# Selective-scan kernel: scans of 513 columns from a constant zero, the carried state in a column of the input

## The chip, the cores and the metric

The kernel runs on one core of one Trainium2 chip. The metric is device microseconds of one execution: the median of three runs. The core has five engines that work side by side and meet only at semaphores: PE (TensorE, matmuls), DVE (VectorE), ACT (ScalarE), POOL (GpSimd) and SP, which here only issues DMAs. Each of them takes its own instructions strictly in the order in which they were written.

## The reference

Two layers over an input of 4 x 512 x 4096 (batch, channels, positions). The first is a selective scan (Mamba) with residual, the second a linear attention with residual. The scan is run for each of four groups of 128 channels:

```python
dt = softplus(einsum(dt, dt_proj_w) + dt_proj_b)        # 256 inner channels
A = -exp(A_log)                                         # 256 x 16 states
def step(h, inp):
    dt_t, B_t, C_t, x_t = inp
    dA = jnp.exp(dt_t[:, :, None] * A)
    h = dA * h + (dt_t * x_t)[:, :, None] * B_t[:, None, :]
    y = jnp.einsum('bds,bs->bd', h, C_t)
    return h, y
```

In the second layer q and k pass a relu, `kq` is the sum over positions of k times q, and the output is `v @ kq`, normed, through an output matrix, plus the residual. Between them stand group norms and layer norms.

## The kernel before, in words

**Tiling.** A step is one image `b`, one tile `t` of T = 512 positions and one group `c` of 128 channels: 4 x 8 x 4 = 128 steps, with `c` innermost. In a step there are 256 inner channels with 16 states each, so 4096 recurrences over 512 positions. They are cut into 8 groups, one for each pair of half `e` and quarter `q` of the states. In a group, 128 partitions hold 32 channels x 4 states, and four blocks `j` of 32 channels stand side by side in the free dimension. So a group has four scans of 128 x 512, and the kernel has 1024 groups and 4096 scans. The carried state `st[:, c, e, q, j]` is needed four steps later, by the next tile of the same channels.

**A group, in two slots.** `slot(g)` writes half a group: two scans. The instructions of a group are these.
- `decay(k)` (L713, ACT): `dA = exp(d_all * a)`, 128 x 512, into PSUM. It is written three scans ahead (`LEAD = 3`), and each of the three `dA` tiles has a PSUM bank of its own.
- `drive(g)` (L721, POOL): `bx = d_all * b_all` for two scans, two slots ahead, in three buffers.
- The scan (L739, DVE): `h = dA * h + bx` along the 512 columns. It starts from `0.0` in the first tile of an image, and otherwise from the column `st[..., j]`.
- After a group's last scan POOL copies the last columns of the four blocks into `st` (L750) and multiplies the last quarter of `h` by `c_sb` (L751).
- `product` (L759, DVE): the first 384 columns of the four blocks, times `c_all`. It is written after the first scan of the next group.
- `c_row` (L705 through the helper at L124, PE): a bf16 matmul that spreads the row of C over the partitions into `c_all`, 384 columns of a PSUM bank. There is one such bank, so it comes after the product that read it last.
- `fold_states` (L772 through L124, PE): four matmuls that sum the states into `y`.

**The rest.** Each slot ends with `after()`, which writes a piece of everything else: the input projections and the short convolution of the step after next, the softplus and silu (with loads of ACT's tables), the spreading of `dt`, norms, output projections, and the attention of the image before. A credit of matmul work per slot sets how much. The order is written out by hand (`manual_schedule`), and the framework puts in the semaphore waits from the tiles that instructions read and write.

**PSUM.** Eight banks: one for `y`, one for `c_all`, three for `dA`, three for work.

Of the kernel before, what the change touches and what calls it, by code (L numbers as in the profile page):

```python
# [8 lines left out]
F32 = mybir.dt.float32  # L9
BF16 = mybir.dt.bfloat16  # L10
AF = mybir.ActivationFunctionType
ALU = mybir.AluOpType
AX = mybir.AxisListType

P = 128
T = 512
# [8 lines left out]
def kernel(  # L25
# [24 lines left out]
    nc = tc.nc  # L50
    B, C, L = x.shape
    NC = C // P
    NT = L // T
    DI = conv_b.shape[0]
# [3 lines left out]
    CUT = T - T // 4  # L58
    BLK = 32
    KS = P // BLK  # L60
    NQ = NST // KS
    NJ = P // BLK

    const = ctx.enter_context(tc.tile_pool(name="const", bufs=1))
    small = ctx.enter_context(tc.tile_pool(name="small", bufs=2))
    wk = ctx.enter_context(tc.tile_pool(name="wk", bufs=2))
    LEAD = 3

    dram = ctx.enter_context(tc.tile_pool(name="dram", bufs=2, space=bass.MemoryType.DRAM))
    ps_y = ctx.enter_context(tc.tile_pool(name="ps_y", bufs=1, space=bass.MemoryType.PSUM))  # L70
    ps_c = ctx.enter_context(tc.tile_pool(name="ps_c", bufs=1, space=bass.MemoryType.PSUM))
    ps_d = ctx.enter_context(tc.tile_pool(name="ps_d", bufs=LEAD, space=bass.MemoryType.PSUM))
    ps_w = ctx.enter_context(tc.tile_pool(name="ps_w", bufs=3, space=bass.MemoryType.PSUM))


# [45 lines left out]
    def mm(out_, lhsT, rhs, abreast=1, **how):  # L121

        work["mm"] += (0.25 if rhs.dtype == BF16 else 1.0) * rhs.shape[-1] / T / abreast
        nc.tensor.matmul(out_, lhsT, rhs, **how)  # L124
# [3 lines left out]
    def diagonal(out_, w, rhs):  # L128

        for k in range(P // BLK):  # L130
            r = slice(k * BLK, (k + 1) * BLK)
            mm(out_[r, :], w[r, :], rhs[r, :], abreast=P // BLK, start=True, stop=False)
# [56 lines left out]
    for i in range(1, 4):  # L189
        r = slice(i * LANE, (i + 1) * LANE)  # L190
# [10 lines left out]
    fold = const.tile([P, BLK], F32, tag="fold", name="fold")  # L201
    for k in range(KS):
        r = slice(k * BLK, (k + 1) * BLK)
# [18 lines left out]


    w_cv = const.tile([P, NTAP, DI], F32, tag="w_cv", name="w_cv")
    w_x = wk.tile([P, DI], F32, tag="bx", name="w_x", bufs=3)
    nc.scalar.dma_start(w_x, in_w[:, 0:DI])
    conv_bc = wk.tile([P, NTAP, DI], F32, tag="h", name="conv_bc", bufs=2)
    nc.scalar.dma_start(conv_bc, conv_w.partition_broadcast(P))
# [22 lines left out]
    for e in range(NH):  # L251
        r = e * (LANE + NST)
# [17 lines left out]


    bqk = const.tile([P, C], BF16, tag="bqk", name="bqk")
    b_qk = wk.tile([P, C], F32, tag="bx", name="b_qk", bufs=3)
    nc.vector.memset(b_qk, 0.0)
    for i in range(P // LANE):
        nc.scalar.dma_start(
# [6 lines left out]
    for i in (2, 3):  # L283
        r = slice(i * LANE, P)
# [7 lines left out]
    a_t = const.tile([P, NH, NJ, NQ], F32, tag="a_t", name="a_t")  # L292
# [82 lines left out]
    def bc(v, n):  # L375
        return v.unsqueeze(1).to_broadcast([P, n, v.shape[-1]])
# [190 lines left out]
    def shifted_end(f, name):  # L567
        mv = small.tile([P, NC, 2], F32, tag="mv", name=f"mv_{name}", bufs=4)
        for v in range(2):
            nc.vector.tensor_reduce(mv[:, :, v], f[("sum", "square")[v]], AX.X, ALU.add)  # L570
        nc.vector.tensor_scalar(mv, mv, 1.0 / L, None, ALU.mult)
        d2 = small.tile([P, NC], F32, tag="d2", name=f"d2_{name}")
        nc.vector.tensor_tensor(d2, mv[:, :, 0], mv[:, :, 0], ALU.mult)
        nc.vector.tensor_tensor(mv[:, :, 1], mv[:, :, 1], d2, ALU.subtract)
        nc.vector.tensor_tensor(mv[:, :, 0], mv[:, :, 0], f["mv"][:, :, 0], ALU.add)
        return mv
# [96 lines left out]
    JJ = NJ // 2  # L673
    SLOTS = NH * NQ * JJ
    AWAY = (3, 10)

    def place(g):

        n, r = divmod(g, SLOTS)
        e, r = divmod(r, NQ * JJ)  # L680
        return n, e, *divmod(r, JJ)

    b_all, c_all, c_sb, dAs, bxs, hs, ys = {}, {}, {}, {}, {}, {}, {}

    def for_states(dst, rows_, q):

# [5 lines left out]
    def b_row(g):  # L692
        n, e, q, _ = place(g)
        b_all[g // JJ] = wk.tile([P, T], F32, tag="b_all", name=f"b_all_{g}", bufs=3)
        for_states(b_all[g // JJ], fs[n]["b_rows"], q)

    def c_tail(g):
        n, e, q, _ = place(g)
        c_sb[g // JJ] = wk.tile([P, T - CUT], F32, tag="c_sb", name=f"c_sb_{g}", bufs=2)
        for_states(c_sb[g // JJ], fs[n]["c_rows"], q)  # L700

    def c_row(g):
        n, e, q, _ = place(g)
        got = ps_c.tile([P, CUT], F32, tag="c", name=f"c_all_{g}")
        mm(got, sel[:, q, :], fs[n]["parts"], start=True, stop=True)  # L705
        c_all[g // JJ] = got

    def decay(k):

        n, e, q, jj = place(k // 2)  # L710
        j = jj * 2 + k % 2
        dAs[k] = ps_d.tile([P, T], F32, tag="dA", name=f"dA_{k}")
        nc.scalar.activation(  # L713
            dAs[k], fs[n]["d_all", e][:, 0, j, :], AF.Exp, scale=a_t[:, e, j, q : q + 1]
        )

    def drive(g):

        n, e, q, jj = place(g)
        bxs[g] = wk.tile([P, 2, T], F32, tag="bx", name=f"bx_{g}", bufs=3)  # L720
        nc.gpsimd.tensor_tensor(  # L721
            bxs[g], fs[n]["d_all", e][:, 1, jj * 2 : jj * 2 + 2, :], bc(b_all[g // JJ], 2), ALU.mult
        )

    def slot(g, last, after):
        n, e, q, jj = place(g)
        b, t, c = steps[n]
        if g + 2 < last:
            drive(g + 2)
        if jj == 0:  # L730
            if g + 3 * JJ < last:
                b_row(g + 3 * JJ)
            hs[g // JJ] = wk.tile([P, NJ, T], F32, tag="h", name=f"h_{g}", bufs=2)
        elif g + 1 < last:
            c_tail(g + 1)
        h = hs[g // JJ]
        for i in range(2):
            j = jj * 2 + i
            nc.vector.tensor_tensor_scan(  # L739
                h[:, j, :], dAs.pop(2 * g + i), bxs[g][:, i, :],  # L740
                0.0 if t == 0 else st[:, c, e, q, j : j + 1], ALU.mult, ALU.add,
            )
            if 2 * g + i + LEAD < 2 * last:
                decay(2 * g + i + LEAD)
            if i == 0 and jj == 0 and g:
                product(g - 1)
                fold_states(g - 1, last)
        del bxs[g]
        if jj == JJ - 1:
            nc.gpsimd.tensor_copy(st[:, c, e, q, :], h[:, :, T - 1])  # L750
            nc.gpsimd.tensor_tensor(  # L751
                h[:, :, CUT:], h[:, :, CUT:], bc(c_sb.pop(g // JJ), NJ), ALU.mult
            )
        after()

    def product(g):

        own = hs[g // JJ][:, :, :CUT]
        nc.vector.tensor_tensor(own, own, bc(c_all.pop(g // JJ), NJ), ALU.mult)  # L759

    def fold_states(g, last):

        n, e, q, _ = place(g)
        if g + 1 < last:
            c_row(g + 1)
        if q == 0:
            ys[n, e] = ps_y.tile([P, T], F32, tag="y", name=f"y_{n}_{e}")
            diagonal(ys[n, e], dg[:, e, :], fs[n]["xz"][:, 0, e, :])
        h = hs.pop(g // JJ)
        for j in range(NJ):  # L770
            mm(
                ys[n, e][j * BLK : (j + 1) * BLK, :], fold, h[:, j, :],  # L772
                start=False, stop=(q == NQ - 1), abreast=NJ,
            )

# [30 lines left out]
    def attention(b, x1s, stats):  # L806
# [54 lines left out]
        for v in range(NT * SUB):  # L861
            t, u = divmod(v, SUB)
# [4 lines left out]
            for j in range(2):  # L867
                yield from room()
                i = 2 * v + j
# [24 lines left out]

        kqn = wk.tile([P, NC, P], F32, tag="res", name=f"kqn_{b}", bufs=2)
        nc.gpsimd.memset(kqn, 0.0)
        nrm = small.tile([P, NC], F32, tag="nrm", name=f"nrm_{b}")
        nc.vector.tensor_reduce(nrm, kq, AX.X, ALU.add)
        nc.vector.tensor_scalar(nrm, nrm, 1e-6, None, ALU.add)
        nc.vector.reciprocal(nrm, nrm)  # L900
        for i in range(P // HEAD):
            r = slice(i * HEAD, (i + 1) * HEAD)
# [22 lines left out]
        gr, _, ngm = norm  # L925
# [46 lines left out]
        for o in range(NC):  # L972
            for k in range(P // BLK):
                r = slice(k * BLK, (k + 1) * BLK)
# [31 lines left out]
    steps = [(b, t, c) for b in range(B) for t in range(NT) for c in range(NC)]  # L1006
    N = len(steps)
    names = [f"{b}_{t}_{c}" for b, t, c in steps]
    fs = [{} for _ in steps]
    xn, pads = {}, {}  # L1010
    norms, stats1, x1s = {}, {}, {}
    st = const.tile([P, NC, NH, NQ, NJ], F32, tag="st", name="st")

    def run(pieces):
        for _ in pieces:
            pass
# [14 lines left out]
    def leave(b, t):  # L1031
        if t == 0:
            stats1[b] = shifted_stats(b)
            x1s[b] = [
                dram.tile([P, NC, T], F32, tag="x1", name=f"x1_{b}_{i}", bufs=3 * NT)
                for i in range(NT)
            ]
        ym = xn[b, t][:, :, NTAP - 1 : NTAP - 1 + T]
        yield from projected(ym, stats1[b], x1s[b][t], b, t)
        if t == NT - 1:  # L1040
            add_to(rest, attention(b, x1s[b], stats1[b]))
# [40 lines left out]
    for g in range(JJ, 3 * JJ, JJ):  # L1082
        b_row(g)
    c_row(0)
    for g in range(2):
        drive(g)
    run(step_inputs(1))
# [6 lines left out]
    with tc.manual_schedule():  # L1094
        credit, seen, mix, held[0], held_x[0] = 0.0, work["mm"], iter(()), 0, 0
        for n, (b, t, c) in enumerate(steps):
            f, nm = fs[n], names[n]
# [9 lines left out]
            for s in range(SLOTS):  # L1107
                def after():
# [62 lines left out]
                    seen = work["mm"]  # L1171

                slot(n * SLOTS + s, N * SLOTS, after)
            fs[n - 1].clear() if n else None
        product(N * SLOTS - 1)
# [64 lines left out]
```

## Time and profile before

| | |
|---|---|
| time, median of three runs | 7947.49 us (7939.57 to 7963.91) |
| the profiled execution | 7963.09 us, span 7961.4 us |
| first scan to last scan | 122.4 to 7493.4 us |
| busy in the span | PE 81%, DVE 88%, ACT 69%, POOL 86% |
| mean granted TensorE clock | 0.897 |
| scan from a column (L739) | 3584 times, mean 1264 ns |
| scan from 0.0 (L739) | 512 times, mean 1203 ns |
| product (L759) | 1024 times, mean 1726 ns |
| exponential (L713) | 4096 times, mean 687 ns |
| `bx` (L721) | 2048 times, mean 2367 ns |

The durations overlap a little where instructions of one engine follow each other at once, so a sum of means is somewhat above the busy time. "Idle before, releaser" is time in which the engine had nothing running, and what ended it. The span falls in three parts: a head of 122 us in which the first inputs are made, the loop over the groups, and a tail of 468 us in which the attention of the last image is finished.

### The profile page before, as it was taken

How to read it: one execution, taken by the hardware profiler on the slowest of the kernel's cores; microseconds unless marked ns; L12 is line 12 of the kernel's file. 1: busy time of each engine (PE TensorE's matmuls, PEld its weight loads, DVE VectorE, ACT ScalarE, POOL GpSimd, SP SyncE). 2: the span in 40 equal slices, each digit the busy share in tenths (PEclk: the TensorE clock that was granted, in tenths of full speed). 3: DMA queues.
4: the chain of work that ended last, by engine and by line, in shares of the span. 5: the costliest groups of instructions: out<-in, count | busy, mean ns of one | idle time of the engine just before them, and what ended most of it. 6: DMA issues, size and time to landing. Idle time of an engine off the chain costs nothing.

```text
span 7961.4 us, 90563 instructions
## 1 busy us (share of the span) xinstructions
PE 6453.6 (81%) x24835; PEld 2120.0 (27%) x24880; DVE 6977.7 (88%) x5766; ACT 5507.6 (69%) x8321; POOL 6880.5 (86%) x4597
## 2 busy tenths in 40 slices
PE   5676777677789888888788888898688888888599
PEld 1121212112223222322222223332122332322144
DVE  5999999999999999989999999998999999988600
ACT  4667777777777777767777777677777777777421
POOL 4999999999999899989999899898999999889600
PEclk7888888888899999998899999899899999999799
DMA  5666666666666666777766666677666666676402
GB/s 154 167 168 166 151 155 159 160 155 167 169 179 162 151 163 159 174 189 175 174 155 171 171 157 161 155 185 189 156 167 163 161 161 159 145 194 180 112 32 90
DMA packets 829184, 1265.87 MB, mean 159 GB/s; under 512 B 183912, under 2 KB 317560, under 8 KB 816384
## 3 DMA queue, kind: packets, MB, share of 16 engines
q1 hardware_dynamic: 804736, 1222.32, 61.1%
q0 software_dynamic: 16896, 33.56, 2.4%
q10 hardware_dynamic: 7040, 4.20, 0.2%
q8 instruction: 195, 3.19, 0.2%
q14 instruction: 317, 2.60, 0.1%
HBM read 1052.78 MB, written 206.57 MB: 158 GB/s over the span
## 4 chain that ended last, share of the span: by engine, by line
DVE 33%; PE 21%; ACT 15%; DMA 12%; issue 8%; SPq 6%; POOL 6%; POOLq 0%; ACTq 0%; DVEq 0%
DVE h L739 22%; DVE h L759 9%; DMA d_all<-d_rows 7%; ACT dA L713 5%; PE pq L124 5%; POOL bx L721 4%; PE pc L124 4%; SPq L688 3%; PE y L124 3%; PE pr L124 3%; SPq L639 2%; DMA c_sb<-c_rows 2%; ACT xz L1048 2%; PE po L124 2%; ACT L1048 1%
## 5 line engine op out<-in xcount | busy, mean ns | idle before, releaser
L721 POOL TENSOR_TENSOR bx<-d_all,b_all 128x1024 f32<-128x1024 f32 x2048 | 4824.7, 2367 | 213.3 <-DVE h L739 195.1
L739 DVE TENSOR_TENSOR_SCAN h<-dA,st,bx 128x512 f32<-128x512 f32 x3584 | 4358.9, 1264 | 358.7 <-ACT dA L713 159.0
L713 ACT ACTIVATE dA<-d_all,a_t 128x512 f32<-128x512 f32 x4096 | 2752.9, 687 | 1568.5 <-DVE h L739 1521.8
L759 DVE TENSOR_TENSOR h<-h,c_all 128x1536 f32<-128x1536 f32 x1024 | 1767.5, 1726 | 0.1
L751 POOL TENSOR_TENSOR h<-h,c_sb 128x512 f32<-128x512 f32 x1024 | 1300.2, 1270 | 190.2 <-DMA c_sb<-c_rows 95.2
L124 PE MATMUL y<-h,fold 128*32 128x512 f32 x8192 | 1271.2, 696 | 71.6 <-POOL h L751 67.4
L124 PE MATMUL c_all<-parts,sel 128*128 128x384 bf16 x1024 | 369.9, 361 | 1123.3 <-DVE h L759 1121.7
L124 PE MATMUL pc<-xn,w_cv 128*128 128x512 f32 x2048 | 1045.7, 645 | 122.8 <-DVE xn L414 62.1
L124 PE MATMUL pq<-w_qk,xa 128*128 128x512 f32 x2048 | 965.5, 604 | 7.9 <-issue 5.3
L739 DVE TENSOR_TENSOR_SCAN h<-dA,bx 128x512 f32<-128x512 f32 x512 | 591.2, 1203 | 90.0 <-ACT dA L713 65.1
L124 PEld LDWEIGHTS <-sel 128*128 128x128 bf16 x1280 | 127.1, 99 | 1762.2 <-DVE h L759 1562.5
L124 PEld LDWEIGHTS pc<-xn,w_cv 128*128 128x128 f32 x2048 | 389.5, 201 | 747.1 <-issue 424.7
L124 PEld LDWEIGHTS pq<-w_qk,xa 128*128 128x128 f32 x2048 | 398.6, 196 | 439.6 <-issue 422.4
L124 PE MATMUL pr<-xb,m 128*128 128x512 f32 x1024 | 485.3, 612 | 7.5 <-DMA xb<-x 3.6
L124 PE MATMUL pp<-xn,w_pr 128*128 128x512 f32 x1024 | 477.7, 597 | 4.8 <-DVE xn L414 4.8
L124 PEld LDWEIGHTS y<-h,fold 128*32 128x32 f32 x8192 | 170.6, 114 | 644.0 <-issue 344.9
L124 PE MATMUL y<-xz,dg 32*32 32x512 f32 x2048 | 337.3, 734 | 0.0
L781 POOL TENSOR_TENSOR xz<-xz 128x512 f32<-128x512 f32 x256 | 325.7, 1272 | 9.2 <-ACT xz L778 9.2
L832 ACT ACTIVATE kq<-pq 128x512 f32<-128x512 f32 x256 | 150.5, 588 | 259.9 <-PE pq L124 259.2
L124 PE MATMUL pd<-xz,w_xp 128*128 128x512 f32 x512 | 323.4, 764 | 7.8 <-ACT xz L1048 7.8
L628 POOL TENSOR_TENSOR dt<-dt,xz 128x1024 f32<-128x1024 f32 x128 | 302.3, 2361 | 24.7 <-ACT dt L620 24.6
L124 PE MATMUL pz<-xn,w_z 128*128 128x512 f32 x512 | 275.4, 631 | 11.7 <-ACT xz L608 8.2
(179 smaller groups left out, 6034.1 us busy)
## 6 DMA issues: line engine op xcount, KB each, us to landing
d_all<-d_rows SPq DMA_DIRECT2D x2048, 256.0 KB, 6.7
b_all<-b_rows SPq DMA_DIRECT2D x4096, 64.0 KB, 2.2
d_rows<-dt SPq DMA_DIRECT2D x256, 512.0 KB, 3.6
c_sb<-c_rows SPq DMA_DIRECT2D x4096, 16.0 KB, 1.8
xs<-in_x_dram SPq DMA_DIRECT2D x32, 1024.0 KB, 6.3
xn<-in_x_dram SPq DMA_DIRECT2D x32, 1024.0 KB, 6.2
xr<-in_x_dram POOLq DMA_DIRECT2D x32, 1024.0 KB, 10.7
x<-xr SPq DMA_DIRECT2D x32, 1024.0 KB, 4.2
```

The lines of the kernel that those rows point to most:

```text
L124: nc.tensor.matmul(out_, lhsT, rhs, **how)
L628: nc.gpsimd.tensor_tensor(f["both"][:, 1], f["both"][:, 0], f["xz"][:, 0], ALU.mult)
L639: nc.sync.dma_start(d[k * BLK : (k + 1) * BLK, v], src)
L688: nc.sync.dma_start(dst[k * BLK : (k + 1) * BLK, :], rows_[q * KS + k, :].partition_broadcast(BLK))
L713: nc.scalar.activation(dAs[k], fs[n]["d_all", e][:, 0, j, :], AF.Exp, scale=a_t[:, e, j, q : q + 1])
L721: nc.gpsimd.tensor_tensor(bxs[g], fs[n]["d_all", e][:, 1, jj * 2 : jj * 2 + 2, :], bc(b_all[g // JJ], 2), ALU.mult)
L739: nc.vector.tensor_tensor_scan(h[:, j, :], dAs.pop(2 * g + i), bxs[g][:, i, :], 0.0 if t == 0 else st[:, c, e, q, j : j + 1], ALU.mult, AL ...
L751: nc.gpsimd.tensor_tensor(h[:, :, CUT:], h[:, :, CUT:], bc(c_sb.pop(g // JJ), NJ), ALU.mult)
L759: nc.vector.tensor_tensor(own, own, bc(c_all.pop(g // JJ), NJ), ALU.mult)
L781: nc.gpsimd.tensor_tensor(f["xz"][:, 1, e, :], f["xz"][:, 1, e, :], f["xz"][:, 0, e, :], ALU.mult)
L832: nc.scalar.activation(qk[i], pq, AF.Relu)
L1048: nc.scalar.activation(fs[n]["xz"], fs[n]["xz"], AF.Silu)
```

## The change

Every scan now covers 513 columns and starts from the constant 0.0. Ahead of `dA` stands a column that is always zero, and ahead of `bx` a column that holds the carried state, so the first column of the scan gives the state itself and the other 512 go on from it. For that
- the three `bx` buffers become one constant tile of three places of 2 x 513 columns;
- the three `dA` tiles and `c_all` become one PSUM tile of four banks, `banks`: `c_all` is columns 0 to 383, and three places of 513 columns stand at 509, 1022 and 1535;
- `h` has 513 columns in a block;
- ACT copies the carried state of a group into `bx` (`carry_in`, one or two copies), and its last columns out into `st` (`carry_out`) right after the group's last scan; in two of eight groups POOL does the copy out, and after the last tile of an image nobody does: POOL clears `st` instead;
- some small setup tiles move to other buffers.

```diff
-    ps_c = ctx.enter_context(tc.tile_pool(name="ps_c", bufs=1, space=bass.MemoryType.PSUM))
-    ps_d = ctx.enter_context(tc.tile_pool(name="ps_d", bufs=LEAD, space=bass.MemoryType.PSUM))
+    ps_d = ctx.enter_context(tc.tile_pool(name="ps_d", bufs=1, space=bass.MemoryType.PSUM))
...
+    RING, ROW = 3, T + 1
+    bx = const.tile([P, RING, 2, ROW], F32, tag="bx", name="bx")
+    banks = ps_d.tile([P, (LEAD + 1) * T], F32, tag="dA", name="banks")
+    dA_slots = banks[:, (LEAD + 1) * T - LEAD * ROW :].rearrange("p (s t) -> p s t", t=ROW)
...
-        got = ps_c.tile([P, CUT], F32, tag="c", name=f"c_all_{g}")
+        got = banks[:, 0:CUT]
...
-        dAs[k] = ps_d.tile([P, T], F32, tag="dA", name=f"dA_{k}")
+        dAs[k] = dA_slots[:, k % LEAD, :]
         nc.scalar.activation(
-            dAs[k], fs[n]["d_all", e][:, 0, j, :], AF.Exp, scale=a_t[:, e, j, q : q + 1]
+            dAs[k][:, 1:], fs[n]["d_all", e][:, 0, j, :], AF.Exp, scale=a_t[:, e, j, q : q + 1]
         )
...
+    def carry_in(g):
+        n, e, q, _ = place(g)
+        got = st[:, steps[n][2], e, q, :].rearrange("p (r i) -> p r i", r=JJ)
+        r = g % RING
+        if r + JJ <= RING:
+            nc.scalar.copy(bx[:, r : r + JJ, :, 0], got)
+        else:
+            for k in range(JJ):
+                nc.scalar.copy(bx[:, (r + k) % RING, :, 0], got[:, k, :])
+
+    def carry_out(g, copy):
+        n, e, q, _ = place(g)
+        b, t, c = steps[n]
+        if t < NT - 1:
+            copy(st[:, c, e, q, :], hs[g // JJ][:, :, T])
...
+        pooled = g % SLOTS in (AWAY[0], AWAY[1] + 1)
         for i in range(2):
             j = jj * 2 + i
             nc.vector.tensor_tensor_scan(
-                h[:, j, :], dAs.pop(2 * g + i), bxs[g][:, i, :],
-                0.0 if t == 0 else st[:, c, e, q, j : j + 1], ALU.mult, ALU.add,
+                h[:, j, :], dAs.pop(2 * g + i), bx[:, g % RING, i, :], 0.0, ALU.mult, ALU.add,
             )
+            if i == 1 and jj == JJ - 1 and not pooled:
+                carry_out(g, nc.scalar.copy)
             if 2 * g + i + LEAD < 2 * last:
                 decay(2 * g + i + LEAD)
+            if i == 0 and jj == JJ - 1 and g + 1 < last:
+                carry_in(g + 1)
...
         if jj == JJ - 1:
-            nc.gpsimd.tensor_copy(st[:, c, e, q, :], h[:, :, T - 1])
+            if pooled:
+                carry_out(g, nc.gpsimd.tensor_copy)
+            if t == NT - 1 and g % SLOTS == SLOTS - 1:
+                nc.gpsimd.memset(st[:, c], 0.0)
...
+    nc.vector.memset(st, 0.0)
+    nc.vector.memset(dA_slots[:, :, 0:1], 0.0)
```

More of the change, by code (lines that the diff above doesn't have):

```diff
@@ L224 @@
     w_cv = const.tile([P, NTAP, DI], F32, tag="w_cv", name="w_cv")
-    w_x = wk.tile([P, DI], F32, tag="bx", name="w_x", bufs=3)
+    w_x = wk.tile([P, DI], F32, tag="res", name="w_x", bufs=2)
     nc.scalar.dma_start(w_x, in_w[:, 0:DI])
@@ L272 @@
     bqk = const.tile([P, C], BF16, tag="bqk", name="bqk")
-    b_qk = wk.tile([P, C], F32, tag="bx", name="b_qk", bufs=3)
+    b_qk = wk.tile([P, C], F32, tag="res", name="b_qk", bufs=2)
     nc.vector.memset(b_qk, 0.0)
@@ L571, in shifted_end @@
         nc.vector.tensor_scalar(mv, mv, 1.0 / L, None, ALU.mult)
-        d2 = small.tile([P, NC], F32, tag="d2", name=f"d2_{name}")
+        d2 = small.tile([P, NC], F32, tag="d2", name=f"d2_{name}", bufs=1)
         nc.vector.tensor_tensor(d2, mv[:, :, 0], mv[:, :, 0], ALU.mult)
@@ L681, in place @@
         return n, e, *divmod(r, JJ)
-    b_all, c_all, c_sb, dAs, bxs, hs, ys = {}, {}, {}, {}, {}, {}, {}
+    b_all, c_all, c_sb, dAs, hs, ys = {}, {}, {}, {}, {}, {}
+    RING, ROW = 3, T + 1
+    bx = const.tile([P, RING, 2, ROW], F32, tag="bx", name="bx")
+    banks = ps_d.tile([P, (LEAD + 1) * T], F32, tag="dA", name="banks")
+    dA_slots = banks[:, (LEAD + 1) * T - LEAD * ROW :].rearrange("p (s t) -> p s t", t=ROW)
     def for_states(dst, rows_, q):
@@ L719, in drive @@
         n, e, q, jj = place(g)
-        bxs[g] = wk.tile([P, 2, T], F32, tag="bx", name=f"bx_{g}", bufs=3)
         nc.gpsimd.tensor_tensor(
-            bxs[g], fs[n]["d_all", e][:, 1, jj * 2 : jj * 2 + 2, :], bc(b_all[g // JJ], 2), ALU.mult
+            bx[:, g % RING, :, 1:], fs[n]["d_all", e][:, 1, jj * 2 : jj * 2 + 2, :], bc(b_all[g // JJ], 2), ALU.mult
         )
+    def carry_in(g):
[12 more added lines that the diff above has]
+            copy(st[:, c, e, q, :], hs[g // JJ][:, :, T])
     def slot(g, last, after):
@@ L732, in slot @@
                 b_row(g + 3 * JJ)
-            hs[g // JJ] = wk.tile([P, NJ, T], F32, tag="h", name=f"h_{g}", bufs=2)
+            hs[g // JJ] = wk.tile([P, NJ, ROW], F32, tag="h", name=f"h_{g}", bufs=2)
         elif g + 1 < last:
@@ L747, in slot @@
                 fold_states(g - 1, last)
-        del bxs[g]
         if jj == JJ - 1:
-            nc.gpsimd.tensor_copy(st[:, c, e, q, :], h[:, :, T - 1])
+            if pooled:
+                carry_out(g, nc.gpsimd.tensor_copy)
+            if t == NT - 1 and g % SLOTS == SLOTS - 1:
+                nc.gpsimd.memset(st[:, c], 0.0)
             nc.gpsimd.tensor_tensor(
-                h[:, :, CUT:], h[:, :, CUT:], bc(c_sb.pop(g // JJ), NJ), ALU.mult
+                h[:, :, 1 + CUT :], h[:, :, 1 + CUT :], bc(c_sb.pop(g // JJ), NJ), ALU.mult
             )
@@ L756, in product @@
     def product(g):
-        own = hs[g // JJ][:, :, :CUT]
+        own = hs[g // JJ][:, :, 1 : 1 + CUT]
         nc.vector.tensor_tensor(own, own, bc(c_all.pop(g // JJ), NJ), ALU.mult)
@@ L771, in fold_states @@
             mm(
-                ys[n, e][j * BLK : (j + 1) * BLK, :], fold, h[:, j, :],
+                ys[n, e][j * BLK : (j + 1) * BLK, :], fold, h[:, j, 1:],
                 start=False, stop=(q == NQ - 1), abreast=NJ,
@@ L896, in attention @@
         nc.gpsimd.memset(kqn, 0.0)
-        nrm = small.tile([P, NC], F32, tag="nrm", name=f"nrm_{b}")
+        nrm = small.tile([P, NC], F32, tag="nrm", name=f"nrm_{b}", bufs=1)
         nc.vector.tensor_reduce(nrm, kq, AX.X, ALU.add)
@@ L1084 @@
     c_row(0)
+    carry_in(0)
     for g in range(2):
```

## The prediction

> **What bounds the kernel now.** I read the page's busy shares first, then its costliest groups, then the loop by stages, then the order of time inside one group.
>
> ```profile
> span 7961.4 us, 90563 instructions
> ...
> PE 6453.6 (81%) x24835; PEld 2120.0 (27%) x24880; DVE 6977.7 (88%) x5766; ACT 5507.6 (69%) x8321; POOL 6880.5 (86%) x4597
> ...
> L721 POOL TENSOR_TENSOR bx<-d_all,b_all 128x1024 f32<-128x1024 f32 x2048 | 4824.7, 2367 | 213.3 <-DVE h L739 195.1
> L739 DVE TENSOR_TENSOR_SCAN h<-dA,st,bx 128x512 f32<-128x512 f32 x3584 | 4358.9, 1264 | 358.7 <-ACT dA L713 159.0
> L713 ACT ACTIVATE dA<-d_all,a_t 128x512 f32<-128x512 f32 x4096 | 2752.9, 687 | 1568.5 <-DVE h L739 1521.8
> ...
> L739 DVE TENSOR_TENSOR_SCAN h<-dA,bx 128x512 f32<-128x512 f32 x512 | 591.2, 1203 | 90.0 <-ACT dA L713 65.1
> ```
>
> Scans from a column take 1264 ns, those from 0.0 take 1203 ns. ACT waits 1522 us for scans; scans hardly wait for ACT (159 + 65 us). ACT runs ahead.
>
> The stages (columns: length, busy of PE, PEld, DVE, ACT, POOL):
>
> ```profile
> 122.40:7493.40 7371.00, 5968.01 (x23212) 1898.49 (x23240) 6913.61 (x5601) 5370.40 (x8110) 6865.96 (x4577) 0.90 0.67 166
> 7493.40:7961.40 468.00, 427.74 (x1494) 195.76 (x1510) 24.76 (x74) 103.85 (x167) 5.59 (x6) 0.94 0.18 59
> ```
>
> In the loop DVE is busy 94% and POOL 93%: 7371 / 1024 = 7.20 us a group. Head and tail together are 590 us.
>
> One group, in order of time (start, length):
>
> ```profile
> 2999.16 1.73 DVE L759 TENSOR_TENSOR h<-h,c_all 128x1536 f32<-128x1536 f32 x1
> ...
> 3000.81 4.80 DVE L739 TENSOR_TENSOR_SCAN h<-dA,st,bx 128x512 f32<-128x512 f32 x4
> ...
> 3000.95 0.34 PE L124 MATMUL c_all<-parts,sel 128*128 128x384 bf16 x1
> ...
> 3002.12 0.69 ACT L713 ACTIVATE dA<-d_all,a_t 128x512 f32<-128x512 f32 x1 [0.75 <-DVE h L739]
> ...
> 3003.30 0.69 ACT L713 ACTIVATE dA<-d_all,a_t 128x512 f32<-128x512 f32 x1 [0.48 <-DVE h L739]
> ...
> 3004.47 0.69 ACT L713 ACTIVATE dA<-d_all,a_t 128x512 f32<-128x512 f32 x1 [0.48 <-DVE h L739]
> ```
>
> Four scans follow each other without a gap, 1.175 us from start to start (those from 0.0: 1.115). The exponentials and the c_all matmul run **under** them. All of that rests on exponentials made three scans early, each in a tile of its own.
>
> **What the change removes.** 3584 scans lose the column operand: 60 ns each back to back, 215 us. The 513th column costs 1115 / 512 = 2 ns a scan, 9 us. POOL loses some 800 copies of 204 ns.
>
> **What it adds, and where.** ACT gets 1365 copies in and 672 copies out of four or two columns a partition. But the larger thing is not in the list of operations. The three places for dA and c_all are now columns of one tile, and in the program as built each wait is set on the last write to that tile, whichever columns it hit. I compared the waits: before, scan number i waits for exponential number i. After, it waits for exponential number i+2, in 3070 of 4096 scans; and that exponential is the one that waits for scan i-1. The second scan of a group (1023 of them) waits for c_row's matmul instead, which waits for the product; and the product (1023 of 1024) waits for the exponential written just before it. So the head start of three is gone: DVE, ACT, DVE, PE take turns. A chain, with nothing beside it but the other engines' other work.
>
> **The chain of one group.** From single records of the trace: a scan from 0.0 that starts after a wait takes 1224 ns, 1226 with the column; from its end to the start of a waiting exponential 35 ns; an exponential after idle time 692 ns; from its end to a waiting scan 33 ns. That makes 1.986 us, four times: 7.944. The product takes 1.726 back to back, 1.753 after a wait (a scan grows by the same 27 ns). From its end to c_all 57 ns; from a matmul's end to waiting DVE work 47 ns. The c_all matmul itself takes 336 ns in the median when PE was idle under 2 us before it, and 502 ns when it was idle over 5 us (29 records; 500 at 3 to 5 us, 145 records). PE will have 6 us of work in a group of over 10, so I take 502: 0.606 with the handovers. (The page TensorE: Matmul & The Clock Gate of the Trainium skill, Part 1, gives the reason: after an idle window of about 3.4 us the array's clock is halved. That PE would always be warm would make it 0.17 us a group less, 170 us in all.) The copy out stands in ACT's queue ahead of the group's last exponential and waits for its last scan; no row shows such a copy on ACT, the nearest are the accumulator reads of 128x1 (189 ns, 93 behind another instruction) and POOL's copy of the same four columns (204). It adds 0.1 to 0.2; I take 0.1, in 672 of 1024 groups: 0.07. The copies in run under a scan: nothing, as long as the scan covers them.
> Sum: 7.944 + 1.753 + 0.606 + 0.07 = **10.37 us** a group, 10,622 us in 1024.
>
> **What does not fit under the scans.** ACT's other instructions stand between the second and third and between the fourth and the next first exponential. What covers them is one scan with its handovers, 1.29 us, and 0.09 since back-to-back ACT instructions overlap. I counted ACT's instructions in each such gap of the changed program and priced them by their rows back to back. Most gaps hold 0.1 to 1.5 us. Two a step hold more: slot 3 with two table loads (1.283 each), two softplus (0.58) and others, 4.4 us; slot 10 with silu (1.911), two loads and others, 5.15 us. Their surplus is 3.0 + 3.8 us, in 128 steps 868 us; all other gaps give 166. Sum 1034. Even today's trace has such a place:
>
> ```profile
> 3018.24 1.28 ACT L1127 ACT_TABLE_LOAD   x1
> ...
> 3019.53 1.27 ACT L620 ACTIVATE dt<-pt,dtb 128x512 f32<-128x512 f32 x2
> ...
> 3020.82 1.28 ACT L1129 ACT_TABLE_LOAD   x1
> ...
> 3022.11 1.30 ACT L713 ACTIVATE dA<-d_all,a_t 128x512 f32<-128x512 f32 x2
> ...
> 3022.84 1.28 DVE L739 TENSOR_TENSOR_SCAN h<-dA,st,bx 128x512 f32<-128x512 f32 x1 [0.15 <-ACT dA L713]
> ```
>
> DVE's own other work runs while an exponential runs, 0.68 free: 93 norm products of 2.26 us stick out by 1.58, 48 pairs of statistics (1.35) by 0.67: 180 us.
> PE's queue: c_all now starts 0.86 us after the product in the mean, 0.06 in the median, because other matmuls stand ahead. Bounds 0 and 0.86 us a group, 0 to 885 us; with PE busy 50% in place of 81% I take 0.1, 100 us.
> POOL, 6.7 us a group, and the DMAs lie under 10.4 us: nothing.
>
> **Sum.** 590 + 10,622 + 1034 + 180 + 100 = 12,526 against a span of 7961; the runs' median is 0.2% below the profiled run, so **12,510 us**.
>
> **A rule that would cut it otherwise.** In the trace exponentials run during scans with each dA in a bank of its own. PSUM — Partial Sum Buffer of the Trainium skill (section PSUM bank collisions raise a hardware error) wants any two engines kept apart by bank, not by address. Places at 509, 1022 and 1535 straddle banks, so two neighbours share one, while the third place's exponential (1536 to 2047) shares none with the first place. By that rule alone a third of the exponentials could stay under the scan after them, and two thirds of those ahead of the product and of the c_all matmuls could stay hidden: 0.76 + 0.51 + 0.40 us a group less, an estimate of 10,800 us. No run here shows it; the waits as built go further.
>
> **The rivals.** (1) *Faster:* the head start survives. It decides if an exponential ends before the scan ahead of its own does. For it: today's 1522 us of ACT waiting. Against: the built waits. Then 215 us go from DVE, ACT's 2037 copies of at most 0.2 us fit, and POOL's loop falls to 6.7 ms: 7947 - 215 + 9 = 7740. (2) *Part of the chain is open,* so that only half of the 3.65 us a group of exponentials, c_all and handovers is in series (1.83 x 1024 = 1870 us less), or all of ACT's surplus is absorbed (1034 less): 10,640 to 11,480. (3) *PE late:* cold matmuls fill its queue and c_all keeps its 0.86 us: 13,300. (4) *The constant start gains nothing* and the head start holds: 7950.
>
> **How the numbers follow.** The chain 0.86, rival (1) 0.03, (2) 0.06, (3) 0.04, (4) 0.01. The chain's own range takes in no lateness and less surplus (11,900) and 0.7 us of lateness (13,200); it leaves out the rest. A change under about 0.3% could not be told from none. Faster 0.03, same 0.01, slower 0.96.
>
> **What would show it.** Right: scans single, 1.22 us, about 0.76 us of idle time before each with ACT's exponential as releaser, one in four released by PE; DVE busy near 57%, POOL near 55%; c_all near 0.5 us. Wrong: scans in rows of four without gaps, or exponentials under scans. If the time is near 11,500, look at the surplus of slots 3 and 10; if over 13,200, at PE ahead of c_all.

## The result, and the profile after

The changed kernel takes **12,449.9 us** (median of four runs, 12,448.2 to 12,455.87), the kernel before beside it 7948.06 us. The ratio is 1.566, with a 95% interval of 1.5635 to 1.5689. The prediction was 12,510 us in a range of 11,900 to 13,200. The profiled execution of after has a span of 12,446.5 us.

From the page of after: span, busy shares, and the groups that make the loop (line, engine, operation, tiles, shapes, count | busy us, mean ns | idle us before, releaser).

```profile
span 12446.5 us, 93106 instructions
...
PE 7601.4 (61%) x24831; PEld 2344.0 (19%) x24880; DVE 7225.2 (58%) x5768; ACT 5850.0 (47%) x10358; POOL 6692.7 (54%) x3813
...
L760 DVE TENSOR_TENSOR_SCAN h<-banks,bx 128x513 f32<-128x513 f32 x4096 | 5017.8, 1225 | 3525.1 <-ACT banks L716 2925.0
...
L716 ACT ACTIVATE banks<-d_all,a_t 128x512 f32<-128x512 f32 x4096 | 2825.9, 690 | 5284.0 <-DVE h L760 5263.2
L123 PE MATMUL banks<-parts,sel 128*128 128x384 bf16 x1024 | 413.3, 404 | 4123.7 <-DVE h L785 4123.4
L785 DVE TENSOR_TENSOR h<-h,banks 128x1536 f32<-128x1536 f32 x1024 | 1796.2, 1754 | 1187.2 <-ACT banks L716 1187.2
```

Read the idle columns against each other. The scans wait for the exponentials, the exponentials for the scans, the product for an exponential, and the c_all matmul for the product. It is a ring: each waits for the one that waits for it, so all of their durations add up. No engine is near full: DVE went from 88% to 58%, POOL from 86% to 54%, ACT from 69% to 47%.

The loop alone (stretch and length, then busy us of PE, PEld, DVE, ACT, POOL, granted clock, DMA share, GB/s):

```profile
123.50:11979.10 11855.60, 7115.60 (x23208) 2122.54 (x23240) 7161.03 (x5601) 5711.40 (x10144) 6675.39 (x3792) 0.77 0.42 103
```

Head (123.5 us) and tail (467.4 us) are as before. The loop takes 11,855.6 / 1024 = 11.58 us a group where it took 7.20. DVE's busy time in it hardly moved, from 6.75 to 6.99 us a group; its idle time went from 0.45 to 4.58. The waits of DVE in after (engine, tile and line that waits, what for: us in all, times, longest us) say where that sits:

```profile
DVE h L760 <- ACT banks L716: 2925.0, 2848, 48.1
DVE h L785 <- ACT banks L716: 1187.2, 1023, 8.6
DVE h L760 <- PE banks L123: 561.8, 1023, 2.9
```

These sum to 4674 us, or 4.56 us a group: all but 0.02 of the idle time.

The timeline of after (start and length in us, engine, line, operation, and the idle time before it with its releaser) shows slot 10 of a step first, and then one group:

```profile
6001.16 1.91 ACT L1076 ACTIVATE xz<-xz 128x2048 f32<-128x2048 f32 x1
...
6003.09 1.28 ACT L1178 ACT_TABLE_LOAD   x1
6004.39 0.69 ACT L716 ACTIVATE banks<-d_all,a_t 128x512 f32<-128x512 f32 x1
...
6005.11 1.22 DVE L760 TENSOR_TENSOR_SCAN h<-banks,bx 128x513 f32<-128x513 f32 x1 [4.44 <-ACT banks L716]
...
6008.41 0.69 ACT L716 ACTIVATE banks<-d_all,a_t 128x512 f32<-128x512 f32 x1 [1.35 <-DVE h L760]
6009.13 1.75 DVE L785 TENSOR_TENSOR h<-h,banks 128x1536 f32<-128x1536 f32 x1 [0.76 <-ACT banks L716]
6010.94 0.48 PE L123 MATMUL banks<-parts,sel 128*128 128x384 bf16 x1 [10.24 <-DVE h L785]
...
6011.45 1.22 DVE L760 TENSOR_TENSOR_SCAN h<-banks,bx 128x513 f32<-128x513 f32 x1 [0.57 <-PE banks L123]
6012.71 0.69 ACT L716 ACTIVATE banks<-d_all,a_t 128x512 f32<-128x512 f32 x1 [3.61 <-DVE h L760]
...
6013.51 1.23 DVE L760 TENSOR_TENSOR_SCAN h<-banks,bx 128x513 f32<-128x513 f32 x1 [0.83 <-ACT banks L716]
```

Add a start and a length and you have the next start, within some 0.1 us, down the whole group: 6008.41 + 0.69 gives 6009.10, and the product starts at 6009.13; 6009.13 + 1.75 gives 6010.88, and c_all starts at 6010.94. In the kernel before, the exponentials and c_all ran under the scans. The first four lines are a place where ACT has more to do than one scan covers: silu and a table load stand ahead of the exponential, and DVE stands still for 4.44 us.

### The profile page after: what moved, and what is told of

The parts are those of the page before. It is cut to its first block, busy times and chain, and to the rows that moved or that the text cites. A ratio compares the mean times of both kernels' runs of the same rounds, so it can differ in the third digit from the quotient of the medians.

```text
span 12446.5 us, 93106 instructions
## 1 busy us (share of the span) xinstructions
PE 7601.4 (61%) x24831; PEld 2344.0 (19%) x24880; DVE 7225.2 (58%) x5768; ACT 5850.0 (47%) x10358; POOL 6692.7 (54%) x3813
## 5 line engine op out<-in xcount | busy, mean ns | idle before, releaser
L760 DVE TENSOR_TENSOR_SCAN h<-banks,bx 128x513 f32<-128x513 f32 x4096 | 5017.8, 1225 | 3525.1 <-ACT banks L716 2925.0
L723 POOL TENSOR_TENSOR bx<-d_all,b_all 128x1024 f32<-128x1024 f32 x2048 | 4814.1, 2351 | 2663.9 <-DVE h L760 2592.7
L716 ACT ACTIVATE banks<-d_all,a_t 128x512 f32<-128x512 f32 x4096 | 2825.9, 690 | 5284.0 <-DVE h L760 5263.2
L123 PE MATMUL banks<-parts,sel 128*128 128x384 bf16 x1024 | 413.3, 404 | 4123.7 <-DVE h L785 4123.4
L785 DVE TENSOR_TENSOR h<-h,banks 128x1536 f32<-128x1536 f32 x1024 | 1796.2, 1754 | 1187.2 <-ACT banks L716 1187.2
L777 POOL TENSOR_TENSOR h<-h,c_sb 128x512 f32<-128x512 f32 x1024 | 1210.0, 1182 | 1679.1 <-ACT st L743 886.3
L123 PE MATMUL y<-h,fold 128*32 128x512 f32 x8192 | 1612.7, 871 | 3.6 <-DVE h L785 3.6
L123 PE MATMUL pc<-xn,w_cv 128*128 128x512 f32 x2048 | 1246.8, 751 | 315.4 <-DVE xn L413 150.7
L743 ACT COPY st<-h 128x4 f32<-128x4 f32 x672 | 132.3, 197 | 768.9 <-DVE h L760 766.6
L123 PE MATMUL y<-xz,dg 32*32 32x512 f32 x2048 | 422.6, 909 | 0.0
L123 PE MATMUL pd<-xz,w_xp 128*128 128x512 f32 x512 | 406.2, 938 | 7.8 <-ACT xz L1076 7.8
L807 POOL TENSOR_TENSOR xz<-xz 128x512 f32<-128x512 f32 x256 | 323.6, 1264 | 3.2 <-ACT xz L804 3.2
```

Source lines behind the costliest of these rows:

```text
L716: nc.scalar.activation(dAs[k][:, 1:], fs[n]["d_all", e][:, 0, j, :], AF.Exp, scale=a_t[:, e, j, q : q + 1])
L723: nc.gpsimd.tensor_tensor(bx[:, g % RING, :, 1:], fs[n]["d_all", e][:, 1, jj * 2 : jj * 2 + 2, :], bc(b_all[g // JJ], 2), ALU.mult)
L743: copy(st[:, c, e, q, :], hs[g // JJ][:, :, T])
L760: nc.vector.tensor_tensor_scan(h[:, j, :], dAs.pop(2 * g + i), bx[:, g % RING, i, :], 0.0, ALU.mult, ALU.add,)
L777: nc.gpsimd.tensor_tensor(h[:, :, 1 + CUT :], h[:, :, 1 + CUT :], bc(c_sb.pop(g // JJ), NJ), ALU.mult)
L807: nc.gpsimd.tensor_tensor(f["xz"][:, 1, e, :], f["xz"][:, 1, e, :], f["xz"][:, 0, e, :], ALU.mult)
```

## The experiments

The theory is that the lost head start is the whole loss: places that are columns of one tile make each scan wait for the exponential written last, and c_all in the same tile adds a turn of PE. The rivals are a cost of what else the change does (513 columns, the constant start, ACT's copies and their place in the queue) and a cost of the places themselves (banks that are straddled or shared). Each ratio below is to the kernel before, in the same set of runs.

**One tile, nothing else (e2).** The kernel before, with its three bank-sized places as columns of one PSUM tile:

```diff
-    ps_d = ctx.enter_context(tc.tile_pool(name="ps_d", bufs=LEAD, space=bass.MemoryType.PSUM))
+    ps_d = ctx.enter_context(tc.tile_pool(name="ps_d", bufs=1, space=bass.MemoryType.PSUM))
...
+    banks = ps_d.tile([P, LEAD * T], F32, tag="dA", name="banks")
...
-        dAs[k] = ps_d.tile([P, T], F32, tag="dA", name=f"dA_{k}")
+        dAs[k] = banks[:, (k % LEAD) * T : (k % LEAD + 1) * T]
```

> The kernel before, with one edit: the three dA places, each still 512 columns and exactly one bank, are columns of one PSUM tile of three banks. No 513th column, no copies on ACT, c_all in its own tile. My theory (waits are set on the last write to the tile, and that takes the head start): scan, exponential, scan take turns except under the product: 0.76 us three times a group and scans at their isolated 1.28 us, 8.95 us a group, with some 890 us of ACT's surplus, 180 of DVE's other work and 590 of head and tail: about 10800 us (10400 to 11200). Rival (columns that straddle banks, or ACT's copies, are what is slow): 7950 us.

Measured: 10,909.33 us, ratio 1.371 (1.3685 to 1.374). Its group of scans from a column:

```profile
L740 DVE TENSOR_TENSOR_SCAN h<-banks,st,bx 128x512 f32<-128x512 f32 x3584 | 4590.6, 1281 | 2719.9 <-ACT banks L714 2680.9 <-PE pd L124 9.8 <-POOL st L751 9.0
```

The same computation on three places of one bank each, with no copies on ACT and no 513th column, loses 2952 us against the 7956.87 us of before in its set. Each place still has a bank of its own, so no shared or straddled bank is needed for this part of the loss. The trace shows the wait itself: at the start of 4094 of the 4096 scans of e2 the exponential for the scan two further on has already ended, and so it is in after. In before that holds for 675 scans.

**A head start of one and of two (e8, e9).** If what is lost is the head start, then taking it away openly, with a tile for each place, must give the same. The kernel before, with one line changed (in e9 it is `LEAD = 2`):

```diff
-    LEAD = 3
+    LEAD = 1
```

> The kernel before with LEAD = 1: one dA tile of one bank, exponentials written one scan ahead. Nothing is shared, but a scan and the exponential of the next one must take turns, as in the run with three places in one tile (10909 us). My theory (the loss is the head start and nothing about the tile, its banks or the memory): the same chain, 10900 us, within 100. Rival (something about places in a common tile costs of itself): clearly under 10800 us.

> The kernel before with LEAD = 2: two dA tiles. It shows whether the two places in the runs with c_all of its own, with own places and in their control cost anything. My theory (one scan of 1.2 us covers an exponential of 0.69, but not ACT's table loads): 7960 to 8400 us. Rival (two places are already the loss seen there): about 10000 us.

Measured: e8 10,920.37 us, ratio 1.3725 (1.3697 to 1.3752); e9 8687.29 us, ratio 1.0918 (1.0896 to 1.094). The scans of e8:

```profile
L739 DVE TENSOR_TENSOR_SCAN h<-dA,st,bx 128x512 f32<-128x512 f32 x3584 | 4591.1, 1281 | 2724.4 <-ACT dA L713 2692.7 <-POOL st L750 9.0 <-PE pd L124 8.1
```

Set this beside e2's line: 1281 ns in both, 2719.9 and 2724.4 us idle, and times 0.1% apart. Three places in one tile behave as one place. That settles the main step. What e9 adds was a miss: two places cost 0.73 ms, above the 450 us that was the most expected. Its scans wait 730 us for exponentials where those of before wait 224, and 208 us for POOL's work on `h` and `st` where before they wait 10. So the third place is worth something beyond covering one exponential. The 367 waits for exponentials last 2.0 us in the mean, longer than one exponential; it seems that the third place takes up the lumps in ACT's other work, but that was not tested. What the waits for POOL come from was not separated.

**c_all out of the tile (e3).** The changed kernel, with c_all in a bank and tile of its own; the banks then leave room for two places instead of three:

```diff
-    LEAD = 3
+    LEAD = 2
...
+    ps_c = ctx.enter_context(tc.tile_pool(name="ps_c", bufs=1, space=bass.MemoryType.PSUM))
...
-        got = banks[:, 0:CUT]
+        got = ps_c.tile([P, CUT], F32, tag="c", name=f"c_all_{g}")
```

> The changed kernel with c_all in a bank and tile of its own again, and two dA places (LEAD = 2) in one tile of three banks to make room for it. My theory (c_all's share of the chain is the exponential ahead of the product and the matmul ahead of the second scan, 0.76 + 0.61 us a group and part of ACT's surplus): about 10850 us (10500 to 11250). Rival (the exponentials alone make the loss, c_all's waits were covered): 12300 to 12450 us.

Measured: 10,808.8 us, ratio 1.3586 (1.3559 to 1.3613). Its group of scans:

```profile
L761 DVE TENSOR_TENSOR_SCAN h<-banks,bx 128x513 f32<-128x513 f32 x4096 | 5010.7, 1223 | 3251.8 <-ACT banks L717 3200.3 <-issue 18.3 <-PE pc L124 10.0
```

The scans' wait for c_all is gone. So the two shared things split the loss: the places in one tile about 2.9 ms (with the rest of the change in it; e2, without that, loses 2.95), c_all in that tile another 1.64 ms (12,449.9 - 10,808.8), 1.60 us a group. That this tile has two places and not three should not matter, since e2 and e8 show that places of one tile behave as one.

**The copies out on POOL (e4).** The changed kernel, with every copy out on POOL and none on ACT:

```diff
-        pooled = g % SLOTS in (AWAY[0], AWAY[1] + 1)
+        pooled = True
```

> The changed kernel with every copy of the state out of h on POOL, as before the change, in place of ACT in six of eight groups. My theory (such a copy costs the chain about 0.1 us in 672 groups): 12385 us, 0.5% under the changed kernel. Rival (the copies on ACT, which stand ahead of the exponentials, are a main part of the loss): under 11800 us.

Measured: 12,405.29 us, ratio 1.5597 (1.5571 to 1.5623), 45 us (0.4%) less than after. The copy out is a small term of the chain and no cause of the loss.

**The constant start alone, the copies out on ACT alone, both (e1, e5, e10).** Three variants of the kernel before, all with its three tiles. e1 and e10 leave out the carried state: they show what the start from a column costs and could not replace the kernel.

e1 has the first edit, e5 the second, e10 both.

```diff
-                0.0 if t == 0 else st[:, c, e, q, j : j + 1], ALU.mult, ALU.add,
+                0.0, ALU.mult, ALU.add,
```

```diff
+            if i == 1 and jj == JJ - 1 and g % SLOTS not in (AWAY[0], AWAY[1] + 1):
+                nc.scalar.copy(st[:, c, e, q, :], h[:, :, T - 1])
...
-            nc.gpsimd.tensor_copy(st[:, c, e, q, :], h[:, :, T - 1])
+            if g % SLOTS in (AWAY[0], AWAY[1] + 1):
+                nc.gpsimd.tensor_copy(st[:, c, e, q, :], h[:, :, T - 1])
```

> The kernel before, with all scans started from the constant 0.0; the carried state is left out (POOL still copies it out). My theory (the loss comes from the waits on the shared tile, and the constant start itself is worth about 60 ns a scan): 3584 scans x 60 ns = 215 us less if DVE alone binds, less where POOL (93% of the loop) takes over: 7735 to 7850 us. Rival (the constant start is worth nothing): 7950 us.

> The kernel before with one part of the change alone: in six of eight groups ACT, not POOL, copies the last columns of h into st, behind the last scan and ahead of the exponential written there. My theory (the waits are what costs; a copy on ACT is covered by the head start of three, and POOL, 93% busy in the loop, gets 768 x 0.2 = 154 us free): the same or faster by up to 100 us, 7850 to 7960. Rival (a copy in ACT's queue that waits for the scan holds up the exponentials even with the head start): 8000 us or more.

> The kernel before with all scans from 0.0 (the carried state is left out) and in six of eight groups ACT in place of POOL copying the last columns out. Scans from 0.0 alone gave 0.94% where 215 us were at stake. My theory (POOL became the bound; 154 us of its copies go to ACT): 7780 to 7850 us, 1.2 to 2.1% under the kernel before. Rival (the rest of the gain was lost elsewhere, in PE's or ACT's waits): 7880 us, as with the scans alone.

Measured: e1 7881.34 us, ratio 0.9906 (0.9891 to 0.992); e5 7952.58 us, 0.999 (0.9981 to 0.9999); e10 7880.74 us, 0.9902 (0.9886 to 0.9919). e5 came as expected; e1 lies 31 us above its range, and e10 came out at its rival's number. The copy on ACT costs nothing while ACT runs ahead. The constant start did take its time from DVE: the scans' mean falls from 1264 to 1204 ns and DVE's busy time by 202 us. But only about 75 us (0.94%) reach the end. The rest turned into waits. The two waits of the scans in e1 (what for: us in all, times, longest us):

```profile
DVE h L739 <- POOL bx L721: 139.2, 127, 5.0
DVE h L739 <- PE y L124: 86.1, 85, 5.6
```

The same two in e10, where they change places:

```profile
DVE h L739 <- PE y L124: 163.0, 144, 5.0
DVE h L739 <- POOL bx L721: 95.2, 86, 5.1
```

In before these two are 78.0 us (POOL) and 90.8 us (PE). A faster DVE waits for POOL; where POOL is relieved of copies too, it waits for PE, and the time is the same. The loop before is so nearly balanced that much of the time saved on one engine reappears as waiting for another. Which of them holds the end was not settled: the expectation that POOL alone does fell with e10.

**A head start, with the change otherwise kept (e6, e7).** e6 is the changed kernel with two places in tiles of their own and c_all in its own bank. A place of 513 columns in a tile of its own takes two PSUM banks. With a bank for `y`, one for c_all and the three for work kept, only one such place fits; the other is in SBUF. To make room, `b_all` has two buffers in place of three.

```diff
-    banks = ps_d.tile([P, (LEAD + 1) * T], F32, tag="dA", name="banks")
-    dA_slots = banks[:, (LEAD + 1) * T - LEAD * ROW :].rearrange("p (s t) -> p s t", t=ROW)
+    dA_slots = [
+        ps_d.tile([P, 2 * T], F32, tag="dA", name="dA_psum")[:, 0:ROW],
+        const.tile([P, ROW], F32, tag="dA_sbuf", name="dA_sbuf"),
+    ]
...
-        got = banks[:, 0:CUT]
+        got = ps_c.tile([P, CUT], F32, tag="c", name=f"c_all_{g}")
```

e7 is its control: the kernel before with exactly these places, at 512 columns, from the column, with POOL's copy.

> The changed kernel (513 columns, constant zero, copies on ACT) with the sharing taken away: two dA places (LEAD = 2), one in a PSUM tile of two banks, one in an SBUF tile, each its own tile; c_all in its own bank; b_all two buffers and loaded two groups ahead, to make room. My theory (with places of their own the waits go back to the scan's own exponential): scans in rows without gaps again, 1.12 us from start to start out of PSUM, and 7800 to 8700 us, the upper end if scans with both inputs in SBUF disturb POOL. Rival (513 columns, straddled banks or the copies make the loss themselves): over 11000 us.

> The kernel before with the same two dA places as in the run with own places (512 columns; one in PSUM, one in SBUF, LEAD = 2, b_all two buffers), scans from the column, the copy out on POOL: what the places alone cost. My theory: 7950 to 8800 us, and the run with own places 50 to 200 us under this one, by the 60 ns a scan and POOL's lost copies. Rival (the 513th column and ACT's copies cost more than the constant start gains): the run with own places is slower than this one.

Measured: e6 10,095.83 us, ratio 1.2689 (1.2669 to 1.2709); e7 10,047.79 us, 1.2636 (1.2618 to 1.2654). Both far above what was expected. The scans of e6:

```profile
L763 DVE TENSOR_TENSOR_SCAN h<-dA_sbuf,bx 128x513 f32<-128x513 f32 x2048 | 4696.1, 2293 | 0.0
...
L763 DVE TENSOR_TENSOR_SCAN h<-dA_psum,bx 128x513 f32<-128x513 f32 x2048 | 2458.9, 1201 | 575.3 <-issue 180.6
```

The head start did come back: no idle time before the scans from SBUF, DVE busy 89%. But DVE is now busy with scans that are nearly twice as long when both inputs lie in SBUF. e7, without any of the change, has the same:

```profile
L743 DVE TENSOR_TENSOR_SCAN h<-dA_sbuf,st,bx 128x512 f32<-128x512 f32 x1792 | 4061.4, 2266 | 0.0
```

So the pair does not tell what the change would be worth with its head start of three; between themselves, under this slower DVE, the edits of the change come to 48 us more, where 50 to 200 us less were expected. A version with three places of 513 columns in separate PSUM tiles was not tried: at two banks each, beside `y` and c_all, they leave no bank for work. No complete version clearly faster than the kernel before came out of the runs; e5, the nearest, is 0.1% below it.

## Why the prediction was right, point by point

**The waits.** The step from which everything followed, that the places lose their head start because they are columns of one tile, is shown by e2 and e8, and the turn of PE by e3. It came from the waits of the built program; the list of operations alone would have given the first rival's 7740.

**The bank rule.** PSUM — Partial Sum Buffer of the Trainium skill (section PSUM bank collisions raise a hardware error) separates engines by bank; by that alone the estimate was 10,800 us. The 12,449.9 us measured are the built waits' number, and e2 loses its time with each place in a bank of its own. By that estimate two thirds of the exponentials ahead of the product would have stayed hidden; in after 1023 of 1024 wait for an exponential (1187.2 us), whichever place it writes. What straddled banks would cost with the waits gone was not tried.

**The terms.** A scan after a wait was put at 1226 ns and measures 1225, an exponential at 692 and 690, the product at 1753 and 1754. From the third scan of a group to the fourth it was to be 1.986 us, and the median is 1.985. The copy out was taken at 0.1 us: from the fourth scan to the next it takes 2134 ns in the median with the copy on ACT and 2039 ns with it on POOL, so 95. Two terms missed, and that they nearly cancelled was luck:
- c_all was put at 502 ns; its median is 476 and its mean 404, the handover to the scan 37 where 47 was taken. Its lateness behind the product is 108 ns in the mean (54 in the median, before 864), where the 57 and the extra 100 us had allowed about 155. Together some 0.15 us a group less than predicted, about 160 us. The 502 ns were read at c_all matmuls before which PE had been idle for over 5 us. In after only 341 of 1024 came after so long a pause, and their median is 479 ns; the 299 that came after less than 2 us have a median of 323. So the matmul does slow down with the idle time before it, as forecast, but not every one of them has that idle time.
- The second scan to the third takes 2053 ns in the median and the fourth to the next 2039 even without ACT's copy, 67 and 53 ns above 1.986. In a group that is 0.12 us more, about 125 us. The scans that end these stretches open a slot, and nearly all of the third and most of the first wait on two or more semaphores in the trace, the others on one; that this is the reason is only argued.

**ACT's surplus.** By place in the step, the eight groups take 10.67, 11.04, 13.42, 10.89, 10.61, 14.40, 10.80 and 10.82 us. The sum gave 10.37 + (166 + 180 + 100) / 1024 = 10.81 for a group without a large surplus; the six such groups average 10.80. The third and the sixth stick out by 2.6 and 3.6 us, where 3.0 and 3.8 were predicted. In 128 steps that is 0.6 x 128 = 77 us less, about the distance between the loop predicted (12,526 - 590 = 11,936) and measured (11,856).

**The rivals.** The first, third and fourth are excluded by the time. So is the second, and the waits say why: no part of the chain is open, since the three waits hold nearly all of DVE's idle time. But its number was not absurd: with c_all out of the tile (e3) the time is 10,809.

**A price in it that does not hold.** The first rival and the removal term put the constant start at 215 us. Alone it brought about 75 (e1). The forecast did not suffer, since the chain was priced with scans from a constant (1226 ns) and has no term of 215 us; a forecast of *faster* by it would have. In a ring it should count in full, which is an estimate from two rows: e2's scans from a column take 1281 ns in the mean, after's 1225.

## What to carry to other kernels

Before counting instructions, see what the program as built waits for: places that are rotated to let one engine run ahead are worth their number only if the framework tracks each by itself. Here that took a tile for each; columns of one tile behaved as one place. Where engines take turns in a ring, the busy shares all fall; here the sum of single durations and handovers gave the time to within a per cent, partly because two errors cancelled. In a loop where two engines are above 90%, take an operation's saving as an upper bound: here about a third of it reached the end.

## What the runs showed of the hardware that was not expected

**A scan with both inputs in SBUF gets in POOL's way, and POOL in its.** Two neighbouring lines of e6's timeline:

```profile
6016.62 2.35 POOL L726 TENSOR_TENSOR bx<-d_all,b_all 128x1024 f32<-128x1024 f32 x1
...
6016.93 3.12 DVE L763 TENSOR_TENSOR_SCAN h<-dA_sbuf,bx 128x513 f32<-128x513 f32 x1
```

POOL's instruction ends at 6018.97, 2.04 us after the scan began, and the scan goes on 1.08 us longer, a little less than the length of one alone (the 163 scans from SBUF in e6 that met no POOL instruction take 1213 ns in the mean). Its time reads as a wait for POOL and then the work. With dA in PSUM the same scan has a mean of 1201 ns under the same POOL. POOL loses less: its `bx` instruction takes 2455 ns in the mean in e6 and 2351 in after, at most 3403. So the statement at the start that the engines meet only at semaphores does not hold for DVE and POOL here. SBUF — State Buffer of the Trainium skill (section SBUF: two separate sides) says that an operation of VectorE with two SBUF inputs and one of GpSimd that reads SBUF lock each other out for a whole instruction. The runs agree with it; for this scan the wait comes to 1.1 us in the mean (2293 against 1201 ns).

**The third place is worth 9%.** Exponentials need 0.69 us and scans 1.2, so two places looked nearly enough; they took 1.0918 of the time of three.
